# A new instruction order for a two-layer attention and feed-forward kernel: first norm's root on GpSimd, two stores on ScalarE, one more unit with its own silu table

## The chip, the cores and the metric

The kernel runs on one core of a Trainium2 chip. A core has five engines that run their own instruction streams: TensorE (PE, matrix products; PEld is its weight loads), VectorE (DVE), ScalarE (ACT, activation functions read from tables), GpSimd (POOL) and SyncE (SP, which here issues DMA transfers). They meet at semaphores. The metric is device time in microseconds (us), the median of a few runs.

## The reference

Two layers, applied one after the other to an input of 4 batches, 1024 tokens and 128 features. In both, x becomes x + attention(norm(x)) * silu(feed-forward(norm(x))).

- Layer norm: subtract the mean, divide by the root of the variance plus 1e-5.
- First attention: 16 heads of 8 features, a causal window of 64 tokens, scores q k / sqrt(128) plus a slope per head times distance, softmax, weighted values.
- First feed-forward: 8 experts are mixed per batch. A small gate network gives 8 factors, averaged over the tokens; the two weight matrices (128 x 512 and 512 x 128) and their biases are a base plus the factor-weighted sum of 8 expert matrices; between them stands a tanh-approximated gelu.
- Second attention: over the 4 batches at each token position, 16 heads, with a position bias scaled by a gate, softmax, output projection.
- Second feed-forward: silu(x W1 s1) * (x W2 s2), then two 512 x 512 layers with an exact gelu each, then back to 128 features; the weights are ternary and every output has a scale.

```
x = x + attention0(layernorm(x)) * silu(experts(layernorm(x)))
x = x + attention1(layernorm(x)) * silu(ternary_ffn(layernorm(x)))
```

## The kernel before

**Units.** The first layer's work is cut into eight units of 512 tokens, numbered in the order in which they are worked: `UNITS = ((0, 0), (0, 1), (1, 0), (1, 1), (2, 0), (3, 0), (2, 1), (3, 1))`, batch and half. The second feed-forward works on units of the same kind; the second attention on slices of 128 positions over all four batches.

**Order.** Every step is a small function that emits instructions for one or a few engines, registered under a short name. The string `ORDER` lists the steps as words: `s.02` is step `s` with arguments 0 and 2. A loop calls them in that order, and each engine executes its own instructions in the order in which they were emitted. Nothing reorders them later; what an engine waits for is settled by the buffers that its instructions read and write. The strings in `PLACES` say which buffer of a ring each tile gets, in order of use.

**Two parts.** A bar in `ORDER` divides it. The words ahead of the bar are the prologue: the whole attention of unit 0, and a test (`VN`, `CK`, `VP`, `VF`) whose result is a flag that all engines read before a branch. Behind the branch stands the same remainder twice, for a fast form and an exact form; the runs take the fast form. The remainder is called the body here.

**The prologue's steps.** `ls` takes statistics, `lp` the reciprocal root, `n` scales, `k` transposes on TensorE, `K` copies to the normalised input (ScalarE). `0` is a matmul on zeros that keeps TensorE running. `q` makes query, key and value products, `m` and `M` write four masked copies of the query (first 128 columns, then the rest, on ScalarE), `kc` stores the keys, `kp` the keys and values of the unit before (POOL), `v` stores the values (DVE). `s` makes a tile of scores in PSUM, for which there is a single buffer that the query product shares; `x` is the exponential on ScalarE, `o` weighs the values, `c` copies, `p` transposes, `d` divides. `A`, `AR`, `B`, `BP`, `C` make the gate factors, `D` and `H`/`HD` the mixed biases, `E` adds one expert matrix to the mixed weights (DVE). `RW` makes two small row weights for that bias. `CK.0` to `CK.3` sum the low bits of the ternary weights, one on DVE and three on ScalarE; their data come by DMA at the start.

**The body's steps.** `f`, `F`, `g`, `G`, `GS`, `r` are the first feed-forward, its silu and the residual. `T` loads expert weights from HBM (SP queue), `L.1` loads the second half of x, and SP issues in written order. `wa`, `wb` are the two gated products of the second feed-forward; `W` the activation, `U` and `V` the products around it, `WH`, `WL` its split in two parts; `ha`, `hb`, `hg`, `hH`, `hL` the first square layer, `ia`, `ib`, `ig`, `gH`, `gL` the second, `j` and `J` the output and its silu. `a` to `ay` are the second attention, `jt`, `y`, `Y` turn the gate, multiply, add and store.

**Tables.** ScalarE's functions lie in sets, and an activation from another set needs a load first. Exp and Tanh stand in the same set here; Silu, exact Gelu and the tanh-approximated Gelu each have another. A unit outside `DIRECT` computes silu from Tanh and one more DVE product (`U`); a unit in `DIRECT` uses Silu and has no `U`.

```
DIRECT = (3, 6, 7)
...
            if u in DIRECT:
                ACT.activation(sl, made["pw1", u, c], AF.Silu, scale=v("w1s", c))
                return
            ACT.activation(sl, made["pw1", u, c], AF.Tanh, scale=halved[:, 0, c:c + 1])
```

Of the kernel before, what the change touches and what calls it, by code (L numbers as in the profile page):

```python
# [52 lines left out]
def constants():  # L53
# [26 lines left out]
    0. ls.00 lp.00 n.00 0. ls.10 0. 0. k.00 0. K.00 q.0 m.00 m.03 m.02 M.00 m.01 M.03 lp.10 VN. M.01 kc.0 M.02 n.10 FI.  # L80
    CK.0 A.00 k.10 RW. v.01 kp.0 v.00 s.00 K.10 x.00 A.01 AR.01 AR.00 v.02 B.0 s.01 H.0 BP.0 o.00 C.0 CK.3 E.00 E.01
    E.02 E.03 E.04 ls.30 lp.30 D.0 x.01 s.02 o.01 CK.1 x.02 HD.0 s.03 n.30 E.05 CK.2 c.01 p.01 VP. x.03 E.06 o.02 VF.
    E.07 o.03 c.03 k.30 d.01 K.30 p.03 d.03 | T.00 f.10 f.00 ls.20 F.00 lp.20 T.01 q.1 f.11 n.20 F.10 L.1 T.10 kp.1 m.10
    f.01 kc.1 k.20 v.10 F.11 m.13 F.01 f.02 A.11 K.20 A.10 F.02 AR.11 T.12 f.12 m.11 m.12 f.03 E.08 E.09 E.0a E.0b E.0c
    AR.10 s.10 E.0d E.0e f.13 v.11 B.1 E.0f ls.60 F.12 F.03 BP.1 g.00 g.01 C.1 lp.60 T.11 x.10 v.12 s.11 E.10 n.60 F.13
    E.11 g.10 G.0 o.10 T.13 x.11 GS.0 E.12 E.13 s.12 E.14 E.15 E.16 E.17 x.12 T.14 g.11 r.0 ls.40 o.11 S.1 E.18 s.13
    c.11 G.1 f.20 x.13 lp.40 ls.01 p.11 lp.01 o.12 o.13 E.19 k.60 D.1 d.11 T.15 E.1a n.01 F.20 c.13 S.0 n.40 f.21 E.1b
    k.01 K.60 T.16 q.2 K.01 XH.0 F.21 f.30 ls.70 A.21 E.1c kc.2 m.20 m.22 k.40 E.1d T.24 F.30 AR.21 m.21 kp.2 XL.0 K.40
    f.31 T.17 lp.70 F.31 m.23 f.22 F.22 A.20 AR.20 ls.50 n.70 f.23 F.23 E.1e f.32 v.20 E.1f v.22 wa.00 p.13 F.32 lp.50
    B.2 W.00 wa.01 T.25 S.2 W.01 s.20 d.13 T.20 U.00 wb.00 U.01 BP.2 wb.01 C.2 f.33 V.00 wa.02 x.20 V.01 v.21 F.33 H.1  # L90
    E.20 s.21 W.02 HD.1 o.20 wa.03 E.28 E.21 U.02 GS.1 wb.02 n.50 W.03 V.02 g.20 wb.03 S.4 x.21 WH.00 WH.01 T.21 E.29
    r.1 g.21 U.03 V.03 E.22 T.22 E.23 G.2 k.50 s.22 WH.02 WH.03 k.70 WL.00 x.22 ha.00 K.70 o.21 E.24 T.26 E.25 E.2a c.21
    s.23 K.50 p.21 ha.01 x.23 GS.2 WL.01 WL.02 kp.3 o.22 o.23 c.23 d.21 ls.11 E.2b WL.03 hb.00 hg.00 hH.00 hb.01 hg.01
    q.3 hH.01 hL.00 S.3 hL.01 ha.02 hb.02 m.30 m.31 kc.3 p.23 m.33 m.32 hg.02 A.31 d.23 hH.02 v.31 hL.02 r.2 E.2c s.30
    v.30 g.30 ls.21 AR.31 A.30 x.30 AR.30 ha.03 hb.03 lp.21 s.31 hg.03 B.3 BP.3 v.32 T.30 n.21 E.2d C.3 U.30 g.31 lp.11
    E.30 k.21 T.34 x.31 K.21 o.30 hH.03 G.3 s.32 x.32 XH.2 XL.2 hL.03 o.31 n.11 wa.20 W.20 T.23 wa.21 E.26 wa.22 U.60
    c.31 U.20 W.21 W.22 s.33 o.32 p.31 E.27 x.33 U.21 U.22 wb.20 ia.00 d.31 wb.21 kp.4 o.33 GS.3 V.20 T.27 wa.23 WH.20
    E.31 V.21 c.33 ib.00 E.38 W.23 WL.20 ig.00 E.39 gH.00 T.35 U.23 WH.21 q.4 D.2 T.31 gL.00 ia.01 kc.4 p.33 ib.01 m.40
    m.42 m.43 m.41 wb.22 d.33 WL.21 ig.01 H.2 v.40 U.61 r.3 HD.2 v.42 s.40 x.40 wb.23 V.22 WH.22 gH.01 V.23 ia.02 ib.02
    s.41 WH.23 v.41 H.3 x.41 gL.01 L.2 WL.22 ig.02 ia.03 HD.3 ha.20 E.32 WL.23 E.3a ib.03 ig.03 hb.20 s.42 hg.20 E.2e  # L100
    E.2f o.40 E.33 T.32 hH.20 E.3b hL.20 o.41 gH.02 gL.02 gH.03 x.42 ha.21 ha.22 hb.21 D.3 gL.03 hb.22 T.33 c.41 ha.23
    hg.21 E.34 E.35 hb.23 ls.31 s.43 hH.21 hg.22 hH.22 hL.21 o.42 hg.23 j.00 hL.22 hH.23 hL.23 p.41 f.40 E.36 x.43 d.41
    j.01 z. j.02 T.36 E.37 lp.31 f.41 o.43 F.40 F.41 T.37 kp.5 c.43 U.70 j.03 f.42 q.5 F.42 J.00 kc.5 m.50 f.50 f.43
    v.50 v.52 F.50 m.52 n.31 F.43 g.40 k.31 g.41 m.51 ia.20 m.53 K.31 E.3c G.4 s.50 GS.4 p.43 ia.21 v.51 x.50 ib.20 E.3d
    ig.20 d.43 gH.20 r.4 ia.22 ls.41 gL.20 ib.21 ig.21 ib.22 ig.22 gH.21 gL.21 o.50 gH.22 gL.22 lp.41 s.51 f.51 f.52
    F.51 n.41 F.52 E.3e f.60 F.60 E.3f k.41 K.41 f.61 F.61 f.62 f.63 F.62 f.53 XH.4 XL.4 F.63 wa.40 W.40 F.53 g.50 x.51
    U.40 wb.40 g.51 V.40 G.5 wa.41 U.62 wa.42 W.41 U.41 W.42 U.42 s.52 wa.43 wb.41 x.52 V.41 wb.42 V.42 W.43 o.51 WH.40
    s.53 c.51 o.52 WH.41 WH.42 WL.40 wb.43 U.43 V.43 WL.41 WL.42 ia.23 x.53 p.51 o.53 GS.5 d.51 WH.43 WL.43 a.00 c.53
    ib.23 aq.00 p.53 kp.6 av.00 ig.23 d.53 gH.23 gL.23 r.5 q.6 ha.40 m.60 k.11 K.11 hb.40 ha.41 kc.6 hg.40 hH.40 m.62
    m.63 hb.41 hg.41 m.61 j.20 v.61 j.21 j.22 j.23 ls.51 lp.51 hL.40 n.51 v.60 hH.41 k.51 hL.41 J.20 K.51 XH.5 s.60 v.62  # L110
    g.60 XL.5 g.61 x.60 wa.50 W.50 wa.51 W.51 s.61 o.60 x.61 U.50 U.51 wa.52 G.6 wb.50 wb.51 V.50 V.51 s.62 wb.52 W.52
    WH.50 wa.53 U.52 a.01 WL.50 V.52 WH.51 WL.51 aq.01 wb.53 x.62 WH.52 W.53 av.01 XH.1 s.63 x.63 U.53 a.02 V.53 ha.42
    XL.1 wa.10 aq.02 av.02 W.10 U.10 hb.42 ha.43 wb.10 hb.43 V.10 hg.42 WL.52 hH.42 hL.42 hg.43 hH.43 o.61 wa.11 WH.53
    hL.43 W.11 a.03 WL.53 U.31 aq.03 ia.40 ib.40 WH.10 U.11 av.03 ag.0 c.61 ig.40 aG.0 wa.12 ap.0 W.12 wa.13 o.62 U.12
    o.63 kp.7 ia.41 W.13 U.13 ib.41 ia.42 gH.40 gL.40 GS.6 as.0 ib.42 ig.41 gH.41 ia.43 gL.41 ib.43 ig.42 gH.42 gL.42
    ig.43 gH.43 a.10 aq.10 av.10 ha.50 hb.50 p.61 gL.43 hg.50 hH.50 c.63 ha.51 hb.51 hg.51 d.61 hH.51 hL.50 p.63 hL.51
    d.63 q.7 a.11 v.71 WL.10 ae.0 ha.52 kc.7 hb.52 v.70 a.12 m.70 m.73 av.11 aq.11 hg.52 ha.53 hb.53 m.71 an.0 m.72
    aq.12 av.12 r.6 hH.52 a.13 ls.61 hg.53 ad.00 lp.61 s.70 hL.52 n.61 av.13 aq.13 j.40 x.70 j.41 ad.01 j.42 wb.11 v.72
    j.43 hH.53 V.11 hL.53 ag.1 s.71 wb.12 U.32 x.71 ia.50 WH.11 o.70 ap.1 V.12 s.72 aG.1 x.72 wb.13 ib.50 as.1 o.71
    WH.12 WL.11 c.71 s.73 V.13 o.72 ae.1 an.1 ad.02 ia.51 WH.13 XH.3 ib.51 x.73 ad.03 a.21 ig.50 ad.10 gH.50 ad.11 a.20  # L120
    ig.51 ad.12 av.20 p.71 o.73 WL.12 d.71 av.21 gH.51 gL.50 a.22 a.23 aq.20 gL.51 aD.10 XL.3 ad.13 wa.30 W.30 f.70
    aD.11 wa.31 ia.52 aq.21 aq.22 J.40 W.31 aq.23 wb.30 ag.2 ib.52 av.22 f.71 c.73 ig.52 a.30 ia.53 av.23 f.72 ap.2 F.70
    F.71 ib.53 gH.52 f.73 av.30 V.30 p.73 aG.2 at.1 as.2 aD.01 gL.52 F.72 F.73 g.70 aD.00 WL.13 ig.53 g.71 aq.30 wa.32
    wb.31 WH.30 a.32 at.0 gH.53 d.73 G.7 W.32 V.31 gL.53 wb.32 a.50 V.32 GS.7 ae.2 a.31 aq.50 av.50 a.33 wa.33 aq.31
    aq.32 j.50 j.51 ha.10 j.52 W.33 ha.11 an.2 WL.30 av.31 r.7 ls.71 WH.31 ad.20 j.53 aq.33 WH.32 J.50 ad.21 ha.12 av.32
    ad.22 av.33 a.40 hb.10 hb.11 lp.71 hg.10 k.61 ad.23 ag.3 ha.13 n.71 ap.3 hH.10 av.40 hg.11 hH.11 K.61 hb.12 wb.33
    hb.13 aq.40 hL.10 hL.11 hg.12 a.51 a.41 XH.6 aT.1 hH.12 aG.3 a.42 hg.13 V.33 hL.12 aq.51 k.71 hH.13 av.41 hL.13
# [20 lines left out]

DIRECT = (3, 6, 7)


LAST = (7, 3)
# [4 lines left out]

PLACES = {  # L160
    "big": (
        "0123456781234065782103645708325764125376087641376254734170182658734287401652858215874871530216153602"
        "74815703626850741"
    ),
    "ps_M": (
# [982 lines left out]
```

## Time and profile before

| | |
|---|---|
| time, median of 3 runs | 413.28 us (412.82 to 413.73) |
| the profiled execution | 415.04 us, of which the span from first to last instruction is 413.2 |
| granted TensorE clock, mean | 0.987 |
| PE, ScalarE, DVE, POOL busy | 398.1, 351.5, 325.7, 167.7 us |
| table loads on ScalarE | 71 of 1.283 us |
| read from HBM, written | 23.52 MB, 2.10 MB |

The page gives the busy time of each engine as a share of the span, the chain of work that ended last, and groups of instructions by source line: how many, the busy time, the mean time of one in ns, and the idle time of the engine just before them with what ended it. A timeline line has the start in us from the span's beginning, the duration, the engine, line, operation and tiles, and in brackets the idle time before. Because matmuls are pipelined, a busy PE is not PE at its peak. Times in the text are from the span's start unless something else is said. The branch lies between 32 and 36 us.

### The profile page before, as it was taken

Reading aid. Unit: us, or ns where it says so; the run is one execution under the profiler, and the core shown is the slowest. Engines: PE = TensorE matmul, PEld = TensorE weight load, DVE = VectorE, ACT = ScalarE, POOL = GpSimd, SP = SyncE. Lnnn points to the kernel's source line nnn. Section 1 sums busy time; section 2 is a strip of 40 time slices with the busy share of each in tenths; the row PEclk is TensorE's granted clock in tenths of the full one; section 3 lists DMA queues with packets and bytes.
Section 4 is the critical chain, followed back from the end, with each engine's and each line's share of the span. In section 5 each row is a group of like instructions: output and inputs, shape, how many; then the busy total and the mean of one; then the engine's idle time right before and its main releaser. Section 6 shows DMA issues by size and latency. Waiting matters only on the chain.

```text
span 413.2 us, 11394 instructions
## 1 busy us (share of the span) xinstructions
PE 398.1 (96%) x4800; PEld 283.2 (69%) x4800; DVE 325.7 (79%) x703; ACT 351.5 (85%) x491; POOL 167.7 (41%) x186
## 2 busy tenths in 40 slices
PE   7879999999999999999999999999999999999992
PEld 3446576577777676767777677666787776778881
DVE  6786989897679776653465596999899999999992
ACT  2875997999989999998988988878996999976972
POOL 2101034437422520031633362447556572675472
PEclk9978999999999999999999999999999999999997
DMA  8916663323114160000000000000000000000013
GB/s 282 389 62 216 243 195 117 102 103 116 43 54 149 36 205 3 2 2 2 2 2 3 2 2 0 2 3 2 2 0 1 2 1 0 2 0 27 0 72 116
DMA packets 8892, 26.43 MB, mean 64 GB/s; under 512 B 1248, under 2 KB 2048, under 8 KB 8448
## 3 DMA queue, kind: packets, MB, share of 16 engines
q1 hardware_dynamic: 8112, 23.79, 16.6%
q10 hardware_dynamic: 720, 1.84, 1.2%
q8 instruction: 39, 0.64, 0.7%
q14 instruction: 21, 0.17, 0.1%
HBM read 23.52 MB, written 2.10 MB: 62 GB/s over the span
## 4 chain that ended last, share of the span: by engine, by line
PE 79%; DVE 11%; ACT 4%; issue 3%; POOL 1%; DVEq 0%; POOLq 0%; ACTq 0%
PE ps_M L826 21%; PE ps_S L614 8%; PE ps_O L667 7%; PE ps_M L710 7%; PE ps_M L727 7%; PE ps_M L770 6%; PE ps_M L919 3%; PE ps_M L866 3%; PE ps_S L604 3%; DVE big L813 2%; PE ps_V L546 2%; PE ps_M L364 2%; PE ps_S L543 2%; PE ps_M L544 2%; DVE vb L971 2%
## 5 line engine op out<-in xcount | busy, mean ns | idle before, releaser
L826 PE MATMUL ps_M<-big,l1h 128*128 128x512 f32 x512 | 134.1, 405 | 0.6 <-DVE big L813 0.3
L826 PEld LDWEIGHTS ps_M<-big,l1h 128*128 128x128 f32 x512 | 93.8, 188 | 25.4 <-issue 3.2
L652 ACT ACTIVATE big<-ps_S 128x2048 f32<-128x2048 f32 x32 | 60.3, 1884 | 12.0 <-PE ps_S L614 11.5
L813 POOL TENSOR_TENSOR big<-t2k,big 128x512 fp32r<-128x512 f32 x32 | 42.3, 1332 | 57.1 <-ACT big L802 51.4
L813 DVE TENSOR_TENSOR big<-ps_M,big 128x512 fp32r<-128x512 f32 x63 | 42.4, 684 | 15.8 <-ACT big L842 11.3
L614 PE MATMUL ps_S<-big,k 32*64 32x256 f32 (+1 forms) x768 | 37.3, 472 | 1.1 <-issue 1.1
L527 DVE SCALAR_TENSOR_TENSOR mw<-tw,gr,mw 128x512 f32<-128x512 f32 x42 | 36.2, 871 | 1.8 <-DMA tw<-in_tw 1.5
L667 PEld LDWEIGHTS ps_O<-big,vb 128*32 128x32 f32 x2048 | 31.3, 113 | 8.4 <-issue 5.1
L667 PE MATMUL ps_O<-big,vb 128*32 128x64 f32 x2048 | 35.6, 225 | 0.0
L428 POOL TENSOR_TENSOR rstd<-rstd,power 128x4 f32<-128x4 f32 x15 | 15.5, 1032 | 49.1 <-DVE rstd L427 34.7
L1005 POOL TENSOR_TENSOR big<-big 128x512 f32<-128x512 f32 x16 | 23.5, 1476 | 21.0 <-DVE big L995 21.0
L710 PE MATMUL ps_M<-xn,mw 128*128 128x512 f32 x64 | 31.5, 602 | 0.3 <-PE ps_M L684 0.3
L727 PEld LDWEIGHTS ps_M<-mw,big 128*128 128x128 f32 x256 | 30.0, 192 | 2.3 <-issue 2.0
L727 PE MATMUL ps_M<-mw,big 128*128 128x128 f32 x256 | 31.3, 277 | 0.0
L742 POOL TENSOR_TENSOR g<-g,s 128x512 f32<-128x512 f32 x8 | 10.2, 1278 | 51.4 <-DVE s L702 35.3
L770 PE MATMUL ps_M<-xh,l1w 128*128 128x512 f32 x64 | 30.4, 474 | 0.3 <-ACT t2k L781 0.3
L919 PE MATMUL ps_M<-wa,xn 128*128 128x416 f32 x64 | 27.2, 522 | 0.1
L614 PEld LDWEIGHTS ps_S<-big,k 32*64 32x64 f32 x768 | 18.9, 133 | 12.1 <-issue 9.4
L770 PE MATMUL ps_M<-xl,l1w 128*128 128x512 f32 x64 | 25.2, 393 | 0.0
L847 ACT ACTIVATE ps_M<-ps_M,vec 128x512 f32<-128x512 f32 x31 | 20.3, 666 | 5.5 <-PE ps_M L826 5.4
L717 ACT ACTIVATE big<-ps_M,mb 128x512 f32<-128x512 f32 x32 | 21.6, 694 | 2.6 <-PE ps_M L710 2.2
L836 ACT ACTIVATE ps_M<-ps_M,vec 128x512 f32<-128x512 f32 x32 | 21.3, 668 | 2.4 <-PE ps_M L826 1.8
(192 smaller groups left out, 830.2 us busy)
## 6 DMA issues: line engine op xcount, KB each, us to landing
tw<-in_tw SPq DMA_DIRECT2D x24, 512.0 KB, 4.0
big<-in_tw SPq DMA_DIRECT2D x2, 1024.0 KB, 5.8
out<-xn SPq DMA_DIRECT2D x7, 256.0 KB, 2.0
g<-in_l1h ACTq DMA_DIRECT2D x2, 512.0 KB, 6.6
g<-in_l1h SPq DMA_DIRECT2D x2, 512.0 KB, 7.4
x<-in_tw SPq DMA_DIRECT2D x2, 512.0 KB, 5.1
x<-in_x SPq DMA_DIRECT2D x1, 1024.0 KB, 5.0
x<-in_x ACTq DMA_DIRECT2D x2, 256.0 KB, 4.0
```

Source lines behind the costliest of these rows:

```text
L527: DVE.scalar_tensor_tensor(m, part, made["gr", b][:, e:e + 1], base if e == 0 else m, ALU.mult, ALU.add)
L614: PE.matmul(sp[rows, j, :, q0:q0 + n], lhsT=k[r, key:key + W], rhs=qm[r, :, t * P + q0:t * P + q0 + n], start=bool(exact), stop=bool(exact ...
L652: ACT.activation(pr, sp, AF.Exp)
L667: PE.matmul(op[32 * j:32 * j + 32, part, qs], lhsT=vb[:, col:col + 32], rhs=pr[:, j, g, qs], start=(odd + i + g == 0), stop=(odd + i + g = ...
L710: PE.matmul(hp, lhsT=made["mixed", b][0][:, c * P:(c + 1) * P], rhs=xn[:, b, cx], start=True, stop=True)
L717: ACT.activation(made["hid", u][:, c, :], made["f", u, c], AF.Gelu_apprx_tanh, bias=made["mixed", b][2][:, c:c + 1])
L727: PE.matmul(op[:, i, :], lhsT=hid[:, c, i * P:(i + 1) * P], rhs=m2[:, c * D:(c + 1) * D], start=(c + i == 0), stop=(c + i == FC + 2))
L770: PE.matmul(p, lhsT=wt[name][:, c * P:(c + 1) * P], rhs=m, start=(n == 0), stop=(n == len(both) - 1))
L813: engine.tensor_tensor(made[key + "l", u][:, c, :], made[key + "v", u, c], made[key + "h", u][:, c, :].bitcast(F32), ALU.subtract)
L826: PE.matmul(made[name, u, c], lhsT=wt[name][:, i, c * P:(c + 1) * P], rhs=m[:, i, :], start=(n + i == 0), stop=(last and i == FC - 1))
L919: PE.matmul(mp[:, 0:N_ALL], lhsT=xn[:, b, place(sl)], rhs=wa[:, 0:N_ALL], start=True, stop=True)
L1005: POOL.tensor_tensor(pv[:, t:t + 2, 0:2, :], pv[:, t:t + 2, 0:2, :], pv[:, t:t + 2, 2:4, :], ALU.add)
```

## The change

1. Step `lp` for unit (0, 0): a ScalarE square root and a DVE reciprocal give way to the form that all other units have, an addition on DVE and a power of -0.5 on POOL. The constant `eps` goes, and the first ScalarE instruction is a copy instead of a square root.
2. Step `kc` for unit 0 runs on ScalarE, and the two stores of step `RW` too; both were on DVE.
3. `DIRECT` gains unit 1, batch 0's second half. It is the fourth unit whose silu is read from its own table.
4. `ORDER` is new in both parts, and `PLACES` with it. The words are the same; `kp.1` moves from the body into the prologue.

```diff
-    0. ls.00 lp.00 n.00 0. ls.10 0. 0. k.00 0. K.00 q.0 m.00 m.03 m.02 M.00 m.01 M.03 lp.10 VN. M.01 kc.0 M.02 n.10 FI.
-    CK.0 A.00 k.10 RW. v.01 kp.0 v.00 s.00 K.10 x.00 A.01 AR.01 AR.00 v.02 B.0 s.01 H.0 BP.0 o.00 C.0 CK.3 E.00 E.01
-    E.02 E.03 E.04 ls.30 lp.30 D.0 x.01 s.02 o.01 CK.1 x.02 HD.0 s.03 n.30 E.05 CK.2 c.01 p.01 VP. x.03 E.06 o.02 VF.
-    E.07 o.03 c.03 k.30 d.01 K.30 p.03 d.03 | T.00 f.10 f.00 ls.20 F.00 lp.20 T.01 q.1 f.11 n.20 F.10 L.1 T.10 kp.1 m.10
+    0. ls.00 0. lp.00 0. VN. 0. n.00 ls.10 0. lp.10 k.00 K.00 CK.1 q.0 FI. kp.0 n.10 A.00 CK.0 m.00 m.03 M.02 v.00 m.02
+    v.02 m.01 kc.0 M.01 k.10 M.03 M.00 K.10 s.00 A.01 x.00 AR.00 AR.01 v.01 B.0 s.01 BP.0 CK.3 x.01 C.0 o.00 D.0 CK.2
+    E.00 E.01 ls.30 s.02 x.02 RW. lp.30 VP. E.02 E.03 kp.1 E.04 E.05 E.06 o.01 s.03 n.30 VF. c.01 x.03 p.01 o.02 o.03
+    k.30 E.07 d.01 c.03 H.0 HD.0 p.03 d.03 K.30 | f.10 ls.20 q.1 T.00 f.11 L.1 F.10 m.10 lp.20 kc.1 n.20 f.12 m.12 F.11
+    f.00 v.11 v.10 T.01 F.12 f.01 m.13 F.00 v.12 E.08 F.01 k.20 K.20 A.11 m.11 A.10 AR.11 E.09 E.0a s.10 E.0b AR.10 x.10
...
-DIRECT = (3, 6, 7)
+DIRECT = (1, 3, 6, 7)
...
-    eps = const.tile([P, 1], F32, tag="eps", name="eps")
-    POOL.memset(eps, 1e-5)
...
-    ACT.activation(warm, one, AF.Sqrt)
+    ACT.copy(warm, one)
...
-            DVE.tensor_scalar(wb[:, 0, :], rp[:, 0, :], 1.0 / S, None, ALU.mult)
-            DVE.tensor_copy(wb[:, 1, :], rp[:, 1, :])
+            ACT.activation(wb[:, 0, :], rp[:, 0, :], AF.Copy, scale=1.0 / S)
+            ACT.copy(wb[:, 1, :], rp[:, 1, :])
...
             rstd = made["rstd", u, i] = small([P, 4], "rstd")
-            if (u, i) == (0, 0):
-                ACT.activation(rstd, made["mv", u, i][:, :, 1], AF.Sqrt, bias=eps)
-                DVE.reciprocal(rstd, rstd)
-                return
             (POOL if i else DVE).tensor_scalar(rstd, made["mv", u, i][:, :, 1], 1e-5, None, ALU.add)
             POOL.tensor_tensor(rstd, rstd, power, ALU.pow)
...
         def keys_of(u):
+            if u == 0:
+                ACT.activation(keys[:, W:W + U], made["kp", u], AF.Copy, scale=1.0 / math.sqrt(D))
+                return
             DVE.tensor_scalar(keys[:, W:W + U], made["kp", u], 1.0 / math.sqrt(D), None, ALU.mult)
```

## The prediction

> **What bounds the kernel now.** I read the page's busy shares and chain first, then the windows, then the timelines of TensorE and ScalarE up to 36 us.
>
> ```profile
> span 413.2 us, 11394 instructions
> PE 398.1 (96%) x4800; PEld 283.2 (69%) x4800; DVE 325.7 (79%) x703; ACT 351.5 (85%) x491; POOL 167.7 (41%) x186
> PE 79%; DVE 11%; ACT 4%; issue 3%; POOL 1%; DVEq 0%; POOLq 0%; ACTq 0%
> ...
> 13.17:16.58 3.41, 3.16 (x51) 1.84 (x50) 3.41 (x7) 3.07 (x6) 0.00 (x0) 1.00 1.04 387
> 16.58:19.99 3.41, 2.47 (x42) 0.95 (x42) 1.90 (x4) 3.41 (x6) 0.00 (x0) 1.00 1.04 407
> ...
> 23.41:26.82 3.41, 1.80 (x74) 1.22 (x70) 3.18 (x15) 1.98 (x3) 0.66 (x1) 1.00 0.03 7
> 26.82:30.23 3.41, 2.98 (x42) 1.47 (x42) 2.53 (x6) 2.00 (x5) 0.35 (x1) 0.50 0.02 5
> ...
> 200.00:250.00 50.00, 50.00 (x665) 37.22 (x666) 31.14 (x60) 44.01 (x61) 21.97 (x26) 1.00 0.01 2
> 280.00:340.00 60.00, 59.96 (x292) 44.29 (x281) 57.62 (x95) 53.84 (x91) 37.44 (x45) 1.00 0.00 1
> 340.00:370.00 30.00, 28.89 (x133) 21.63 (x132) 29.07 (x45) 26.66 (x45) 16.40 (x16) 1.00 0.00 1
> ```
> A window row gives its length, then the busy us of PE, PEld, DVE, ACT and POOL, then the granted clock. From about 36 us on PE has no gap worth having: 50.00 of 50 and 59.96 of 60, and 1.1 us missing at 340 to 370, where DVE is at 29.07 of 30. The matmuls are the same in number before and after. So the body can give about 1 us and can lose any amount. What can be won lies before 36 us.
>
> ```profile
> 5.88 1.28 ACT L323 ACT_TABLE_LOAD   x1 [5.88 <-DMA x<-in_x]
> ...
> 7.29 0.28 ACT L424 ACTIVATE rstd<-mv,eps 128x4 f32<-128x4 f32 x1
> 9.35 0.59 ACT L446 COPY xn<-ps_M 128x512 f32<-128x512 f32 x1 [1.78 <-PE ps_M L441]
> 11.15 0.89 ACT L581 ACTIVATE big<-ps_S,cst 128x128 f32<-128x128 f32 x3 [1.22 <-PE ps_S L543]
> ...
> 16.41 1.88 ACT L652 ACTIVATE big<-ps_S 128x2048 f32<-128x2048 f32 x1 [0.32 <-PE ps_S L614]
> ...
> 21.88 1.93 ACT L381 ACTIVATE big<-g 128x2048 f32<-128x2048 uint16 x1
> ...
> 25.32 1.88 ACT L652 ACTIVATE big<-ps_S 128x2048 f32<-128x2048 f32 x1 [1.43 <-PE ps_S L614]
> ...
> 30.02 1.88 ACT L652 ACTIVATE big<-ps_S 128x2048 f32<-128x2048 f32 x1 [1.41 <-PE ps_S L614]
> ```
> ```profile
> 24.62 0.65 PE L614 MATMUL ps_S<-big,k 32*64 32x256 f32 x5 [1.09 <-issue]
> ...
> 35.57 0.67 PE L710 MATMUL ps_M<-xn,mw 128*128 128x512 f32 x1 [0.31 <-PE ps_M L684]
> ```
> ```profile
> L652 ACT ACT_TABLE_LOAD x15 | 19.2, 1283 | 0.3
> L428 POOL TENSOR_TENSOR rstd<-rstd,power 128x4 f32<-128x4 f32 x15 | 15.5, 1032 | 49.1 <-DVE rstd L427 34.7 <-DVE shares L507 13.7
> L790 DVE SCALAR_TENSOR_TENSOR t2k<-t2k,ps_M 128x512 f32<-128x512 f32 x20 | 13.3, 682 | 9.4 <-ACT t2k L783 9.3
> ```
> The prologue is a ladder: four score tiles of the first unit, each through PE (about 1.65 us) and then ScalarE's exponential (1.88). The third and fourth exponentials wait 1.4 us each: the third because PE stood in the middle of its scores (24.62, released by nothing but issue), the fourth because PE's clock had been halved at 26.82. The first body matmul starts at 35.57.
>
> **The change, part by part.** *Root.* Before: table load to 7.16, root to 7.57, reciprocal, scaling at 7.81. After: DVE's add (0.17) ends near 5.8, POOL's power takes 1.03 (its row), scaling starts near 7.05. Those 0.76 us are mostly covered by the idle matmuls: five now stand ahead of the transposes instead of four, and the fifth is two warm passes of 0.43, so 7.57 becomes 8.43. Transposes (0.66) end at 9.1, and K.00 starts 0.23 earlier. POOL's second root moves to about 9.6 and is free at 10.7; its keys and value memsets follow, wanted at 15.
>
> *ScalarE's list.* Now K.00 (to 9.7), then CK.1 (row at 21.88: 1.8 and 0.2 for its read). Its data: issued at 2.11 and 7.4 to landing, about 9.5, just in time. It fills the 1.22 us in which ScalarE waited for the query, but costs 2.0: masks start at 11.75 instead of 11.15. Then four masks of 0.255, four of 0.475 and the keys (0.6 by the copy rows; DVE's row was 0.68): done at 15.4 instead of 14.2. The scores need the query's bank, so they wait for the last mask: 15.4, not 14.7. The first exponential starts at 17.1, 0.7 late. The Sqrt load and the Exp load at 14.80 merge into the one at 5.88, which saves 1.3 of ScalarE but nothing on the path, since the exponential waited for PE anyway.
>
> *PE's clock.* PE is idle from 13.9 (second transposes) to 15.4: 13.17 to 16.58 holds 0.73 + 1.18 = 1.91 us of matmuls, where before it held 3.16. The row 1.80 was followed by 0.50 for 6.8 us, the row 2.47 was not; 1.91 is nearest to 1.80, so I take half clock from 16.58 to 23.41. The Trainium skill ("TensorE: Matmul & The Clock Gate", "Why this matters for your kernels") asks only that there be no idle gap over about 3 us; by it nothing would halve here, and neither would it have at 26.82, where the longest gap was 1.5. The trace speaks against it; I keep both.
>
> *The ladder after.* Half clock (score tile 2.77 as at 27.25): exponentials at 17.55; 22.25 (bank free 19.4, two relus, CK.3); then CK.2 to 25.3; 25.85; row weights (2 x 0.28) and a copy; 29.45; then o.03 to 32.4, copy, last transposes 33.5, body from 33.85: 1.7 earlier than 35.57. Full clock: 17.1, 20.9, 24.5, 28.1, body from 32.4: 3.1 earlier. The gain is CK.1 out of the ladder's middle, and neither 1.4 us wait. DVE's share: gr at 22.6, eight expert steps of 0.75, stats, norm and flag to 32.6, still before 33.85. DVE loses the keys and row weights (1.25), which hid under PE.
> *Waits added.* The first scaling on DVE now waits for POOL instead of ScalarE; behind it stand the second half's statistics, whose root has until 10.7. The keys on ScalarE wait for the second projection (11.6, before their turn at 13.2); behind them stand three masks and the copy K.10. POOL's kp.1 copies come before the branch; their reads are over by 24.3, and only a later root stands behind them.
>
> *SP after the branch.* The 2 MB load of x now stands ahead of the second tw2 half, and waits for a DVE write behind one set of statistics, near 36. That half is issued near 36.4 instead of 33.41 and lands near 43.5 instead of 40.2 (the x load ahead of it took 5.0). Its first reader, expert step 0c, comes after some 8 us of DVE work from 36, near 44. Bounds 0 and +1; I take 0, as the second layer's weights are wanted only at g.00, later still.
>
> *Unit (0,1)'s silu.* Four DVE steps of 0.682 go (2.7 us); Tanh 0.687 becomes Silu 0.693. Built in order, the program has 73 table loads instead of 71, 72 of them in the body instead of 69: 3 x 1.283 = 3.85 us of ScalarE. A rule speaks against this: the skill ("ScalarE: Activation LUTs", "What ACT_TABLE_LOAD costs") adds a drain of about 1.38, 2.66 in all. Here the next activation follows its load by 1.30, so the row decides: 3.85, not 8.0. Most of it falls where unit (2,1) is scored, in the 200 to 250 row: ScalarE idle 50 - 44.0 = 6.0. 3.85 fits, 8.0 would not. I take 0 on the path, bounds 0 and +3.85. DVE's relief: at most the 1.1 us that PE lacks at 340 to 370; I take 0, since the four steps stood near 240, where DVE had slack.
> *Order otherwise.* Summing row means in written order, ScalarE's work never exceeds PE's over any stretch by more than 7.0 us (7.1 before), DVE's by 9.0 (11.1 before). I take 0, with bounds -1 and +3. Tail: six sums of 1.34 on POOL instead of five close together; the last is ready near the last multiply as before: 0.
>
> **Sum.** -0.2 (root and warm-up) and -1.5 (ladder) = -1.7. The profiled run took 415.04 (span 413.2 and 1.8 around), 1.8 above the median of 413.28; 1.7 off gives 413.3 profiled, 411.6 for the median.
>
> **The rivals.**
> *Full clock throughout:* the gap at 13.9 does not halve it. For: the page's rule, and 1.91 is over 1.80. Against: the row. -3.1: 410.2.
> *No change:* PE's stop at 24.62 returns. It reads as a late instruction, fetched while loads kept the DMA engines full to about 23; the same place in the program now comes near 24, after them. If it returns, 1.5 of the 1.7 is gone: 413.1.
> *Slower:* the extra loads reach PE. From unit (2,1)'s first exponential to its fourth ScalarE has 25.1 us of listed work against PE's 22.1; the same stretch before had 9.8 against 10.0. PE has a single score bank and cannot score until the exponential ends. It decides from the point where ScalarE enters this stretch less than 3 us ahead of need. For: three loads more, two of them here. Against: 6 us idle there, and a 7.1 excess near 55 us that cost nothing. With all 3.85 on PE: 413.28 - 1.7 + 3.85 = 415.4.
>
> **How the numbers follow.** Main case 0.36 (411.6), full clock 0.12 (410.2), no change 0.20 (413.1), slower 0.32 (415.4; an order this tight loses more easily than it wins). A measurement here tells 0.2%, 0.8 us, from no change. Faster 0.48, same 0.20, slower 0.32. Range 409.6 to 415.6: from full clock with half of DVE's 1.1 to the slower case. The main case alone: 410.5 to 412.4.
>
> **What would show it.** Right: 72 loads after the branch; first exponential near 17.1 to 17.6, third before 26, first body matmul 33 to 34.5; half clock moved to about 16.6; no long issue gap in the third scores; PE over 49.5 of 50 from 200 to 250. Wrong: first body matmul at 35 or later; PE idle behind exponentials or table loads after 200 us; DVE waiting near 44 for the second tw2 half.

## Result and the profile after

| | before | after |
|---|---|---|
| time, median | 412.76 us (412.00 to 413.73, 6 runs) | 415.10 us (414.41 to 415.71, 6 runs) |
| ratio | | 1.0053, 95% interval 1.0033 to 1.0072 |
| the profiled execution | 415.04, span 413.2 | 414.82, span 413.0 |

The changed kernel is slower by 0.5%, although its profiled execution was slightly faster than that of the kernel before. This contradiction leads to the first error of the prediction. One execution, of run 11 below, took 1244.73 us for a reason that the record does not show, and is left out of that run's ratio. First, the page and the window rows after, in the columns of the rows shown above (length, busy us of PE, PEld, DVE, ACT, POOL, granted clock, DMA):

```profile
span 413.0 us, 11393 instructions
PE 396.3 (96%) x4800; PEld 282.1 (68%) x4800; DVE 324.8 (79%) x696; ACT 352.7 (85%) x495; POOL 166.1 (40%) x186
```
```profile
8.05:11.46 3.41, 1.83 (x6) 1.04 (x7) 2.77 (x16) 1.41 (x2) 0.49 (x1) 1.00 1.04 402
11.46:14.88 3.42, 3.42 (x10) 2.00 (x9) 2.61 (x5) 3.42 (x9) 1.53 (x6) 0.50 1.05 334
...
200.00:250.00 50.00, 50.00 (x730) 37.35 (x721) 29.94 (x59) 48.01 (x64) 18.33 (x22) 1.00 0.01 2
...
280.00:340.00 60.00, 59.05 (x327) 44.20 (x326) 57.67 (x98) 50.44 (x89) 36.22 (x39) 1.00 0.00 1
340.00:370.00 30.00, 28.98 (x139) 23.50 (x138) 28.42 (x43) 27.91 (x47) 16.06 (x15) 1.00 0.00 1
```
The totals hardly move. The rows say more: the half clock is at 11.46 to 14.88 and nowhere near 16.58; from 200 to 250 TensorE is full although ScalarE took 4.0 us more there; from 280 to 340 it lacks 0.95 us where it had lacked 0.04. The timeline of ScalarE and TensorE after, at the rungs of the ladder:

```profile
10.05 0.59 ACT L440 COPY xn<-ps_M 128x512 f32<-128x512 f32 x1 [2.84 <-PE ps_M L435]
...
18.14 1.88 ACT L649 ACTIVATE big<-ps_S 128x2048 f32<-128x2048 f32 x1 [0.98 <-PE ps_S L611]
...
25.44 1.88 ACT L649 ACTIVATE big<-ps_S 128x2048 f32<-128x2048 f32 x1 [0.67 <-PE ps_S L611]
...
29.03 1.88 ACT L649 ACTIVATE big<-ps_S 128x2048 f32<-128x2048 f32 x1 [1.01 <-PE ps_S L611]
```
```profile
33.91 1.10 PE L707 MATMUL ps_M<-xn,mw 128*128 128x512 f32 x2 [0.44 <-DVE inv L693]
```
The first body matmul is 1.66 us earlier than the 35.57 of before, the size that was forecast (1.7). Yet the last product of the second feed-forward (`j`) ends at 405.58 instead of 404.82. Its lines, before and after:

```profile
403.80 1.02 PE L862 MATMUL ps_M<-t2k,l1w 128*128 128x512 f32 x2
```
```profile
404.55 1.02 PE L859 MATMUL ps_M<-t2k,l1w 128*128 128x512 f32 x2
```
So the body, counted from one to the other, took 371.67 us instead of 369.25: 2.42 more. Between these ends TensorE's gaps of over 60 ns add up to 3.21 us, before to 1.30. That is 1.91 of the 2.42; the gaps of 60 ns and less add up to 0.04 in both, so the other 0.5 us is not idle time of TensorE. The record does not say what it is. The longest gap after:

```profile
354.46 1.28 ACT L778 ACT_TABLE_LOAD   x1
...
355.76 0.69 ACT L778 ACTIVATE t2k<-ps_M,vec 128x512 f32<-128x512 f32 x1
...
356.50 0.50 PE L767 MATMUL ps_M<-xh,l1w 128*128 128x512 f32 x1 [1.02 <-ACT t2k L778]
...
357.04 1.28 ACT L844 ACT_TABLE_LOAD   x1
```
This is the silu of the last row tile of unit (3,1), `W.73`. One activation stands between two table loads, for gelu, silu and gelu again, and TensorE waits 1.02 us for the bank that this silu reads. The old order has the same single silu between two loads, before:

```profile
355.29 1.28 ACT L781 ACT_TABLE_LOAD   x1
356.63 0.69 ACT L781 ACTIVATE t2k<-ps_M,vec 128x512 f32<-128x512 f32 x1
357.34 1.28 ACT L836 ACT_TABLE_LOAD   x1
```
There TensorE has no gap behind it. What differs is not the pair of loads but what waits behind them.

### The profile page after: what moved, and what is told of

The parts are those of the page before. It is cut to its first block, busy times and chain, and to the rows that moved or that the text cites. A ratio compares the mean times of both kernels' runs of the same rounds, so it can differ in the third digit from the quotient of the medians.

```text
span 413.0 us, 11393 instructions
## 1 busy us (share of the span) xinstructions
PE 396.3 (96%) x4800; PEld 282.1 (68%) x4800; DVE 324.8 (79%) x696; ACT 352.7 (85%) x495; POOL 166.1 (40%) x186
## 3 DMA queue, kind: packets, MB, share of 16 engines
q10 hardware_dynamic: 720, 1.84, 1.3%
## 4 chain that ended last, share of the span: by engine, by line
PE 70%; DVE 15%; ACT 11%; issue 2%; POOL 0%; ACTq 0%; DVEq 0%
PE ps_M L823 19%; PE ps_M L767 7%; PE ps_S L611 6%; PE ps_M L724 6%; PE ps_M L707 6%; PE ps_O L664 6%; PE ps_M L916 2%; PE ps_S L601 2%; DVE big L810 2%; ACT big L649 2%; PE ps_M L863 2%; PE ps_V L540 2%; PE ps_M L538 2%; DVE big L992 2%; PE ps_S L537 2%
## 5 line engine op out<-in xcount | busy, mean ns | idle before, releaser
L823 PE MATMUL ps_M<-big,l1h 128*128 128x512 f32 x512 | 132.2, 402 | 0.0
L823 PEld LDWEIGHTS ps_M<-big,l1h 128*128 128x128 f32 x512 | 94.2, 188 | 24.6 <-issue 3.2
L422 POOL TENSOR_TENSOR rstd<-rstd,power 128x4 f32<-128x4 f32 x16 | 18.8, 1175 | 51.5 <-DVE rstd L421 50.8
L664 PEld LDWEIGHTS ps_O<-big,vb 128*32 128x32 f32 x2048 | 29.9, 110 | 10.2 <-issue 6.7
L611 PE MATMUL ps_S<-big,k 32*64 32x256 f32 (+1 forms) x768 | 35.8, 462 | 0.0
L521 DVE SCALAR_TENSOR_TENSOR mw<-tw,gr,mw 128x512 f32<-128x512 f32 x42 | 35.0, 847 | 0.3
L664 PE MATMUL ps_O<-big,vb 128*32 128x64 f32 x2048 | 34.2, 220 | 0.6 <-ACT big L649 0.6
L739 POOL TENSOR_TENSOR g<-g,s 128x512 f32<-128x512 f32 x8 | 11.4, 1428 | 46.7 <-ACT g L734 34.6
L833 ACT ACTIVATE ps_M<-ps_M,vec 128x512 f32<-128x512 f32 x32 | 21.3, 668 | 7.6 <-PE ps_M L823 7.3
L429 DVE TENSOR_SCALAR nt<-x,mv,rstd 128x128 f32<-128x128 f32 x64 | 20.4, 382 | 2.4 <-POOL rstd L422 2.4
```

The source lines that it names most:

```text
L521: DVE.scalar_tensor_tensor(m, part, made["gr", b][:, e:e + 1], base if e == 0 else m, ALU.mult, ALU.add)
L611: PE.matmul(sp[rows, j, :, q0:q0 + n], lhsT=k[r, key:key + W], rhs=qm[r, :, t * P + q0:t * P + q0 + n], start=bool(exact), stop=bool(exact ...
L664: PE.matmul(op[32 * j:32 * j + 32, part, qs], lhsT=vb[:, col:col + 32], rhs=pr[:, j, g, qs], start=(odd + i + g == 0), stop=(odd + i + g = ...
L823: PE.matmul(made[name, u, c], lhsT=wt[name][:, i, c * P:(c + 1) * P], rhs=m[:, i, :], start=(n + i == 0), stop=(last and i == FC - 1))
L833: ACT.activation(full, full, AF.Gelu, scale=v("h1s", c))
```

## Experiments

All ratios are to the kernel before, with 95% intervals. "Body" and "gaps" are read from each run's one profiled execution as above; the last digit can be off by one from rounding. The same words of the body differ between executions by up to 0.6 us (371.67 and 371.29 in the changed kernel and run 7, 369.91 and 370.49 in runs 10 and 11), so smaller differences of a body are not a result.

**1. The kernel before, once more.** No edit.

> The kernel before, unchanged, profiled a second time. Theory A: the first profiled execution (415.04 us) was an unlucky one, with the half clock at 26.82 and the stop at 24.62 in it, while the usual execution has neither; then this profile has its first body matmul near 33 us, not 35.57, and its span near 411. Theory B: the prologue always takes 35.6 us and the 1.8 us of the first profile lie elsewhere; then the first body matmul is again at 35 to 36. The ratio to itself is 1.000 within 0.2% in both.

Measured: 412.36 us, ratio 0.9994 (0.9975 to 1.0013). Its profiled execution took 412.41 with a span of 410.6, where the one used for the prediction had taken 415.04 and 413.2. Timelines and windows of this execution:

```profile
24.61 0.65 PE L614 MATMUL ps_S<-big,k 32*64 32x256 f32 x5 [1.10 <-issue]
...
33.44 1.95 PE L710 MATMUL ps_M<-xn,mw 128*128 128x512 f32 x4 [0.30 <-PE ps_M L684]
```
```profile
28.90 1.88 ACT L652 ACTIVATE big<-ps_S 128x2048 f32<-128x2048 f32 x1 [0.30 <-PE ps_S L614]
```
```profile
21.17:24.58 3.41, 1.94 (x70) 1.03 (x58) 3.27 (x5) 2.71 (x3) 0.00 (x0) 1.00 0.40 151
```
TensorE's stop at 24.6 is there again, so that one belongs to the kernel. The half clock behind it is not: the clock stays at 1.00, the fourth exponential starts at 28.90 instead of 30.02, and the first body matmul at 33.44 instead of 35.57. The body is 369.17, as it was. The prologue of this execution is thus 2.1 us shorter than that of the profile from which the prediction was worked out. It is also the more frequent kind: of 102 executions of the kernel before that were timed beside the twelve runs, 17 took over 414 us, all of them at a mean granted clock of 0.993 or less, and none of the 60 at 0.995 or more did.

**2. Old prologue, new body.** Against the kernel before, the places where the body begins:

```diff
-    E.07 o.03 c.03 k.30 d.01 K.30 p.03 d.03 | T.00 f.10 f.00 ls.20 F.00 lp.20 T.01 q.1 f.11 n.20 F.10 L.1 T.10 kp.1 m.10
+    E.07 o.03 c.03 k.30 d.01 K.30 p.03 d.03 | f.10 ls.20 q.1 T.00 f.11 L.1 F.10 kp.1 m.10 lp.20 kc.1 n.20 f.12 m.12 F.11
...
-DIRECT = (3, 6, 7)
+DIRECT = (1, 3, 6, 7)
```

> Prologue of before (words, places and code), body of the changed kernel with unit (0,1)'s own silu table. Theory A (the new body order loses, the new prologue gains nothing against the usual execution): ratio 1.004 to 1.006. Theory B (the body is equal and the new prologue loses): 0.999 to 1.001. Theory C (both lose about half): 1.002 to 1.003.

Measured: 415.38 us, ratio 1.0065 (1.0041 to 1.0090), just above theory A's range; body 371.80, with a wait of 1.03 us at 356.85.

**3. New prologue, old body.** Against the changed kernel, likewise:

```diff
-    k.30 E.07 d.01 c.03 H.0 HD.0 p.03 d.03 K.30 | f.10 ls.20 q.1 T.00 f.11 L.1 F.10 m.10 lp.20 kc.1 n.20 f.12 m.12 F.11
+    k.30 E.07 d.01 c.03 H.0 HD.0 p.03 d.03 K.30 | T.00 f.10 f.00 ls.20 F.00 lp.20 T.01 q.1 f.11 n.20 F.10 L.1 T.10 m.10
...
-DIRECT = (1, 3, 6, 7)
+DIRECT = (3, 6, 7)
```

> Prologue of the changed kernel (words, places, POOL root, keys and row weights on ScalarE), body of before, unit (0,1) by Tanh. Theory A: ratio 0.998 to 1.001. Theory B: 1.004 to 1.006. Theory C: 1.002 to 1.003. The forecast's own step, a prologue 1.7 us shorter, would be 0.996.

Measured: 413.09 us, ratio 1.0005 (0.9985 to 1.0025); body 369.26. Runs 2 and 3 together put the whole loss into the body: with the new one the time is that of the changed kernel, with the old one that of the kernel before, whichever prologue stands ahead.

**4. The own table alone, in the old order.**

```diff
-DIRECT = (3, 6, 7)
+DIRECT = (1, 3, 6, 7)
```

> The kernel before with only unit (0,1) added to those that read Silu from its own table: order and places as before, four DVE products fewer, the table loads that the old order then needs. If table loads of ScalarE reach TensorE: 1.28 us for each added load, ratio 1.006 or more for two or three added. If ScalarE's slack near 240 us hides them, as forecast: 0.999 to 1.001.

Measured: 417.79 us, ratio 1.0110 (1.0080 to 1.0141); body 374.64, 5.4 more. In the old order the own table costs more than the whole change does. ScalarE and TensorE at the place, and two windows:

```profile
241.46 1.28 ACT L781 ACT_TABLE_LOAD   x1
...
243.50 6.88 PE L826 MATMUL ps_M<-big,l1h 128*128 128x512 f32 x22 [1.89 <-ACT t2k L781]
```
```profile
240.70:244.11 3.41, 1.52 (x70) 1.26 (x59) 0.00 (x0) 3.37 (x6) 1.98 (x6) 1.00 0.02 5
244.11:247.53 3.42, 3.42 (x10) 2.65 (x9) 2.89 (x3) 1.57 (x3) 0.00 (x0) 0.50 0.00 0
```
The silu of the third row tile waits for a gelu's load, the gelu and its own load; TensorE stands for 1.89 us, and then 3.41 us pass at half clock, in which about 1.7 us of work is lost (3.41 times a half). The half clock belongs to this execution and not to the price: three of the six executions had a mean clock of 0.990 or 0.991 and took 417.32 to 418.01 us, the other three 0.996 or 0.997 and took 417.78 to 418.10. In every profile the clock is also halved for the last 2 to 5 us, so that 0.996 leaves no room for another step of 3.41. TensorE's gaps add up to 3.75 us here, 2.45 more than before; the rest of the 5.4 is not explained for the executions at whole clock.

**5. Tanh in the new order.**

```diff
-    W.10 a.03 WL.53 W.11 av.03 wa.12 c.61 aq.03 ia.40 W.12 x.63
+    W.10 U.10 a.03 WL.53 W.11 U.11 av.03 wa.12 c.61 aq.03 ia.40 W.12 U.12 x.63
...
-    wa.13 as.0 W.13 q.7
+    wa.13 as.0 W.13 U.13 q.7
...
-DIRECT = (1, 3, 6, 7)
+DIRECT = (3, 6, 7)
```

> Edit: the changed kernel with unit (0,1)'s silu back in the exponential's table (Tanh and four DVE steps, moved behind their Tanh in the written list); 72 table loads instead of 73. The body runs from the first body matmul to the last attention output; it was 369.25 us before and 371.67 after. Theory A (the own table is what costs in the new order, as it does in the old one, where it alone gave a ratio of 1.011): body back near 369.5, time near 413.0, ratio to before 1.000 to 1.002. Rival B (the new order itself costs it, wherever the silu takes its table): body 371 to 372, ratio 1.004 to 1.007, and the 1.02 us gap of TensorE at 356.5 is still there. A mixture would show the gap at 356.5 and a body near 370.5.

Measured: 415.71 us, ratio 1.0065 (1.0042 to 1.0089); body 372.99, gaps 3.82, and the 1.02 us at 358.05. Rival B's ratio and its gap hold, and the body is even above its 372: the new order costs this wherever the silu takes its table. The body is 1.3 us longer than with the own table; part of this may be the place of the four returned DVE steps, since TensorE waits for them twice (0.34 at 237.95, 0.18 at 251.74). This run also tells what the own table adds in the new order. It has 71 loads after the branch, the changed kernel 72, the kernel before 69: one load of the three belongs to the own table, and two come with the new order, wherever the silu takes its table.

**6. The last silu beside the third, in the new order.**

```diff
-    W.72 ay.2 aT.3 ig.30 V.71 wa.73 WH.70 WL.70 as.7 ia.31 ia.32 gH.30 ha.60 W.73 ad.40
+    W.72 wa.73 W.73 ay.2 aT.3 ig.30 V.71 WH.70 WL.70 as.7 ia.31 ia.32 gH.30 ha.60 ad.40
```

> Edit: the changed kernel with the last row tile's silu of unit (1,3) (words wa.73 and W.73) moved directly behind the third's, so that it shares its table; 71 loads instead of 73. Theory A (the 1.02 us gap of TensorE at 356.5, where this one activation stands between two table loads of its own, is part of the loss): the gap is gone, body 370.6, time near 414.0, ratio to before 1.002 to 1.004. Rival B (what that gap holds back is made up by slack later, or the two loads only move the wait on): body within 0.4 of 371.67, ratio 1.004 to 1.007, and other gaps stand between 350 and 380.

Measured: 413.61 us, ratio 1.0022 (1.0011 to 1.0033); body 370.43, 1.24 less than in the changed kernel, and no gap between 323 and 396:

```profile
340.00:370.00 30.00, 30.00 (x144) 24.32 (x143) 29.54 (x45) 25.79 (x44) 17.34 (x16) 1.00 0.00 1
```
Theory A holds. Two words moved take two loads away and give back about half of the loss.

**7. The halving behind the first scaling, in the new prologue.** In the changed kernel DVE's next work behind the first root is the word `VN`. The timeline of DVE in the changed kernel:

```profile
7.91 0.17 DVE L368 TENSOR_SCALAR halved<-vec 128x4 f32<-128x4 f32 x1 [1.90 <-DMA vec<-in_vec]
...
8.52 1.11 DVE L429 TENSOR_SCALAR nt<-x,mv,rstd 128x128 f32<-128x128 f32 x4
```
```diff
-    0. ls.00 0. lp.00 0. VN. 0. n.00 ls.10 0. lp.10 k.00 K.00
+    0. ls.00 0. lp.00 0. 0. n.00 VN. ls.10 0. lp.10 k.00 K.00
```

> Edit: the changed kernel with DVE's word that halves the vector (the one that waits 1.90 us for a transfer) moved behind the first scaling. Theory A (that wait is why the first scaling starts at 8.52 instead of the forecast 7.05): the scaling starts near 7.0 and the query copy on ScalarE near 9.3 to 9.6 instead of 10.05; if the chain behind it follows, the first exponential starts near 17.5 instead of 18.14, the first body matmul near 33.4 instead of 33.91, ratio to before 1.003 to 1.005. Rival B (the idle matmuls or the transfer of the keys' weights that ScalarE waits for hold the prologue anyway): first exponential within 0.2 of 18.1, first body matmul within 0.3 of 33.9, ratio 1.004 to 1.007.

Measured: 415.26 us, ratio 1.0060 (1.0039 to 1.0082); body 371.29. DVE's first scaling in this run:

```profile
6.88 1.11 DVE L429 TENSOR_SCALAR nt<-x,mv,rstd 128x128 f32<-128x128 f32 x4 [1.23 <-POOL rstd L422]
```
It now waits for the root, as the forecast had it (7.05); the first exponential starts at 17.19 and the first body matmul at 33.03. In its trace theory A holds. In the time nothing of it can be seen, and the ratio lies in rival B's range: the intervals of this run and of the changed kernel lie over each other, and 0.9 us of one execution's prologue is of the size by which executions differ.

**8. New prologue so mended, old body.** The edits of runs 3 and 7 together, with the body's three PSUM banks renamed (0 to 2, 1 to 0, 2 to 1). Against run 3:

```diff
-    0. ls.00 0. lp.00 0. VN. 0. n.00 ls.10 0. lp.10 k.00 K.00
+    0. ls.00 0. lp.00 0. 0. n.00 VN. ls.10 0. lp.10 k.00 K.00
```

> Edit: the new prologue with the halving moved as in the run before this one, and then the old body (Tanh for unit (0,1), old order), with the body's three PSUM banks renamed so that its first projection does not wait for the bank of the prologue's last product. Theory A (the old body is worth 369.25 wherever it starts, and the prologue ends earlier once its wait is gone): first body matmul near 33.0 to 33.4, body 369.3, ratio to before 0.996 to 0.999. Rival B (the new prologue cannot beat the old one in its usual execution): first body matmul 33.9 to 34.4 as it was, ratio 0.999 to 1.003.

Measured: 412.31 us, ratio 0.9984 (0.9964 to 1.0004); body 369.42, first body matmul 33.86. The body is as theory A had it; the start is as rival B had it, because this execution had half clock from 17.67 to 21.08. Undecided against the kernel before.

**9. Four more words of the new order.** Runs 6 and 7 together, and

```diff
-    ha.00 E.26 kc.3 hb.00 F.33 hg.00 T.30 r.2 ls.21 lp.21 m.30 v.30 v.31 hH.00 hL.00
+    ha.00 E.26 kc.3 hb.00 F.33 hg.00 T.30 r.2 ls.21 lp.21 v.30 v.31 hH.00 m.30 hL.00
...
-    r.4 ig.21 gL.20 gH.21 ls.41 ig.22 gH.22 o.50 f.50 lp.41 gL.21 f.61
+    r.4 ig.21 gL.20 gH.21 ig.22 gH.22 o.50 f.50 gL.21 ls.41 lp.41 f.61
...
-    K.61 wa.31 an.2 V.30 W.31 wb.31 g.71 V.31 wa.32
+    K.61 wa.31 V.30 W.31 wb.31 g.71 V.31 an.2 wa.32
...
-    j.53 W.60 ag.5 af.1 ag.4 WH.33 J.50 wa.61
+    j.53 W.60 J.50 ag.5 af.1 ag.4 WH.33 wa.61
```

> Edit: the changed kernel with the last row tile's silu of unit (1,3) early as before, the halving behind the first scaling, and four words moved so that no short work stands ahead of what TensorE waits for: m.30 behind hH.00, the statistics ls.41 behind gL.21, the normalisation an.2 behind V.31, the silu J.50 ahead of three words. They aim at the gaps of 0.26 (107), 0.33 (182), 0.24 (294) and 0.40 us (323), 1.23 in all. Theory A (the rest of the body's loss is the sum of these small waits): body 370.43 - 1.23 = 369.2, as in the old order; ratio to before 0.998 to 1.000. Rival B (waits only move on to the next word): body 370.0 to 370.6, ratio 1.001 to 1.003.

Measured: 412.64 us, ratio 1.0005 (0.9988 to 1.0022); body 369.82, 0.61 less than in run 6 where 1.23 had been aimed at. The gaps at 107, 294 and 323 are gone or smaller; the one at 182 grew from 0.33 to 0.51, and new ones of 0.12 and 0.33 stand at 110 and 114. Most of it moved on: the gaps counted in the whole body add up to 2.04 us, against 2.20 in run 6. The 0.61 of the body is no larger than the difference between two executions of one body, and the interval overlaps that of run 6. With all these moves the new order cannot be told from the old one; which of the last five brought the ratio from 1.0022 to 1.0005, if any, is open.

**10 and 11. Three words of the old body, with the new prologue and with the old.**

```diff
-    W.70 hH.32 WL.61 a.73 W.71 a.62
+    W.70 WL.61 a.73 W.71 hH.32 a.62
...
-    hg.60 hg.33 hH.33 aD.31 hL.33
+    hg.33 hH.33 hg.60 aD.31 hL.33
...
-    WL.71 an.5 aT.3 aU.3 ib.32 hL.62 af.3 jt.40
+    WL.71 aT.3 aU.3 ib.32 hL.62 an.5 af.3 jt.40
```

> Edit: the new prologue with the late halving and the old body with three words moved: hH.32 behind W.71, hg.60 behind hH.33, an.5 behind hL.62. They aim at the old body's gaps of 0.25 (342), 0.32 (353) and 0.20 us (365). Theory A (a gap of TensorE in the body is worth its length): body 369.42 - 0.77 = 368.7, ratio to before 0.996 to 0.998, under both kernels. Rival B (the waits move on): body 369.2 to 369.5, ratio 0.998 to 1.000.

> Edit: the kernel before with the same three words moved in its body, its prologue as it is. Theory A (the new prologue, with its halving late, is worth no more than the old one in its usual execution, and a gap is worth its length): body 368.5, first body matmul near 33.4, ratio to before 0.997 to 0.999, within 0.001 of the run with the new prologue. Rival B (the prologue's change is worth its 0.4 us or more, as the first body matmul at 33.03 in one execution suggests): this one stays 0.001 to 0.002 above that run.

Measured: with the new prologue 412.34 us, ratio 0.9988 (0.9974 to 1.0002), body 369.91; with the old 412.80 us, ratio 1.0002 (0.9986 to 1.0018), body 370.49. Both bodies are longer than the old one, which no theory had. Two of the three moves made the wait longer: 0.25 us at 342 became 0.44, and 0.32 at 353 became 1.59. Only the 0.20 at 365 is gone. ScalarE and TensorE at the place, in run 10:

```profile
349.18 1.28 ACT L833 ACT_TABLE_LOAD   x1 [1.95 <-PE ps_M L823]
```
```profile
352.54 0.73 PE L823 MATMUL ps_M<-big,l1h 128*128 128x512 f32 x2 [1.59 <-DVE big L810]
```
`hg.60` had been the first of the two gelus, its input was there early, and the load was made while the product for `hg.33` was still running. With `hg.33` first, the load itself waits for that product, 1.95 us, and the bank that the low half behind it gives back is late. The prologue's part agrees with the trace: in run 10 the exponentials start at 17.09, 20.80, 24.39 and 28.08 and the first body matmul at 32.76, in run 11 the latter is at 33.18. That would be 0.4 us for the new prologue; the two ratios lie 0.0014 apart with intervals that overlap, so it is not settled.

**12. The own table in the old order, with the four silus together.**

```diff
-    ag.0 c.61 ig.40 aG.0 wa.12 ap.0 W.12
+    ag.0 c.61 aG.0 wa.12 ap.0 W.12
...
-    ib.41 ia.42 gH.40 gL.40 GS.6 as.0 ib.42 ig.41 gH.41 ia.43 gL.41
+    ib.41 ia.42 GS.6 ig.40 gH.40 gL.40 as.0 ib.42 ig.41 gH.41 ia.43 gL.41
```

> Edit: the kernel before with unit (0,1)'s silu from its own table, and three words (the gelu ig.40, its high and low halves) moved behind the four silus and the small silu GS.6, so that these share one load: 72 loads instead of 74 (71 with Tanh). Theory A (the own table's price in the old order, 1.1%, is the wait of the silu behind a load and a gelu, with TensorE empty for 1.89 us at 243.5 and its clock halved in the 3.41 us that follow): gap and half clock are gone, body near 370.5, ratio 1.002 to 1.005. Rival B (the price is the loads themselves, ScalarE's time, wherever they stand): ratio above 1.007, and gaps of TensorE behind ScalarE elsewhere between 225 and 260.

Measured: 418.02 us, ratio 1.0137 (1.0105 to 1.0170), with two loads fewer than in run 4; body 373.43. TensorE and its window:

```profile
249.02 0.96 PE L919 MATMUL ps_M<-wa,xn 128*128 128x416 f32 x2 [2.52 <-DVE big L813]
```
```profile
247.22:250.63 3.41, 1.61 (x6) 1.15 (x7) 2.88 (x7) 0.70 (x2) 0.00 (x0) 1.00 0.00 0
```
In this execution the wait for the silu is gone, and so is the half clock. But DVE now begins `as.0` at 243.58, before the low half `gL.41`, which stands behind it in the order. Its input was cast by 244.18; DVE comes to it at 248.28, and TensorE waits for that bank: 2.52 us in place of 1.89. And this execution, 415.59 us at a mean clock of 0.997, is the fastest of six: the others took 416.96 to 420.61, longer mostly where the clock was lower, from 0.996 down to 0.984. At 0.996 and more run 12 took 415.59 and 416.96, run 4 417.78 to 418.10. So the grouping gained 1 to 2 us where the clock was whole, and lost it again to half clock that this one trace does not show. Theory A's range is missed; rival B has the ratio, but the long gap stands behind DVE and not ScalarE. That the price is the time for which some bank stays taken is a reading of these two traces, not a test of it.

## Why the prediction was wrong, point by point

**The profiled execution that the sum stood on was not the usual one.** This is the step that failed first. The prediction took 1.7 us off the profiled 415.04 and the same 1.7 off the median of 413.28, as if the 1.8 us between the two were the constant that lies outside the span. But 1.7 to 1.9 us lie outside the span in every execution (413.2 and 415.04; 410.6 and 412.41 in run 1), and the median contains them too. The profiled execution was itself slow: the half clock at 26.82 and most of the fourth exponential's wait of 1.41 (0.30 in run 1) were its own. Against the 33.44 of run 1 the changed kernel's 33.91 is no gain, and runs 2 and 3 show none in the time either. 415.04 lay outside the three runs shown (412.82 to 413.73); the question to ask was which row was its excess.

**The ladder's term had the right working and the wrong start.** The first exponential came at 18.14 instead of 17.55, the third before 26 (25.44). That the first body matmul came at 33.91, beside the 33.85 of the main case, is luck: the half clock of that case was not there, and the four exponentials follow the full-clock rival's steps (17.1, 20.9, 24.5, 28.1) about 1.0 us late. With the halving moved, run 10 follows this ladder within 0.11 us at each exponential, and its first body matmul is at 32.76 for the rival's 32.4.

**The root's term missed a wait.** The root itself was ready at 6.91, as forecast. But `VN`, a word that the diff puts ahead of `n.00`, waits 1.90 us for the vector's transfer, and the scaling started at 8.52 instead of 7.05. The forecast asked what waits behind the scaling and not what the new order puts in front of it.

**Half clock from 16.58 to 23.41 did not come.** It was taken because 1.91 us of matmuls is nearest to the 1.80 of one row. It came from 11.46 to 14.88 instead, behind the window of 1.83 that holds the wait for `VN`. The longest gap of TensorE ahead of 26.82, which the prediction gives as 1.5, is 1.09 by the line at 24.62. The last section returns to the clock.

**The own silu table at 0 had the loads wrong.** The prediction charges all three added loads, 3.85 us, to unit (0,1)'s silu. Run 5 shows that one of them is its own and two come with the order. For the one, 0 fits the trace: ScalarE is at 48.01 in 200 to 250, TensorE full, and the changed kernel is not slower than run 5. In the old order the own table does add three loads (69 to 72 after the branch), and the body is 5.4 us longer, outside the upper bound of 3.85. So neither a count of loads nor ScalarE's idle time gave the price; how it comes to 5.4 is explained only in part. DVE's relief was 0 where it was looked for: in run 4, without the four DVE steps, the old order's gaps of TensorE between 340 and 370 still add up to 1.08 us (1.11 before). The second half of `tw2` cost nothing: DVE's idle time at 44.30 is 0.69 us, and it waits for ScalarE.

**Order otherwise at 0 is the term that decided the sign.** The body measured +2.42 us, within the term's bound of +3. Runs 2, 3 and 5 put this into the order of the body; run 6 returns 1.24 of it with `W.73` beside the third silu. The rest is not pinned down. Gaps of a few tenths, as at 162 and 317, are part of it, 0.5 us of it are no gaps, and the moves of run 9 leave open which of them matter. The forecast compared sums of work over stretches, ScalarE's excess of 7.0 with 7.1 before. Such a sum is blind to the wait at 356.50: no engine is overfull there, one bank's reader stands behind one load too many.

**The rivals.** The slower case said 415.4, close to 415.1, but for another reason: its place, unit (2,1)'s exponentials between 200 and 250, shows no wait at all, and its 1.7 us of prologue gain does not exist against the usual kernel. "PE idle behind exponentials or table loads after 200 us" was named as what would show the forecast wrong, and the line at 356.50 is that. *No change* rested on TensorE's stop at 24.62. The stop is in all six profiles of the old prologue, always in the third scores (0.82 to 1.38 us). In five of the eight of the new one it stands among the row-weight products instead (0.27 to 1.01 us, at 24.85 to 26.31), behind the third scores, where the third exponential does not wait for it. In all eleven TensorE goes on 2.2 to 2.6 us after a transfer of 16 KB on the instruction queue begins (at 22.08 in the profile before). This fits the prediction's reading of a late instruction; no run tested it.

## What to carry to other kernels

Before working out a gain from a stretch of one profiled execution, set its time against the other runs; if it stands above them, find the row that is its excess and take it out first. For a reordered program whose bound engine has no slack, walk along the banks and ask for each who reads it last and what has been put ahead of that reader; sums over stretches don't see it. A table load is priced where it stands: one activation between two loads cost 1.02 us in the new order and nothing that TensorE shows in the old one.

## What the runs showed of the hardware

The granted clock moves in steps of 3.41 us, and the grid of the steps lies elsewhere in each execution: the half clock of the profile before began at 26.82, those of the changed kernel, run 4, run 8 and run 9 at 11.46, 244.11, 17.67 and 15.80. The step before each held little matmul: 1.80, 1.83, 1.52, 1.59 and 0.92 us of 3.41. Run 9's windows:

```profile
12.39:15.80 3.41, 0.92 (x6) 0.48 (x5) 2.40 (x3) 3.41 (x12) 0.00 (x0) 1.00 1.06 369
15.80:19.21 3.41, 3.19 (x41) 1.51 (x41) 1.89 (x3) 1.04 (x3) 0.00 (x0) 0.50 0.99 377
```
Steps on the execution's own grid with 1.94 (run 1), 1.77 (run 10), 1.80 (run 11) and 1.61 us (run 12) were not followed by half clock, so 1.6 to 1.8 us busy of 3.41 went either way in these traces. The longest idle gaps that reach into the steps ahead of the five half clocks were 1.09, 1.39, 1.89, 1.84 and 2.70 us; gaps of 2.28 (run 7) and 2.52 us (run 12) left the clock whole. What else decides is not shown. The Trainium skill ("TensorE: Matmul & The Clock Gate", "What's actually happening") states a free-running window of 3413 ns that does not start with the kernel. The steps agree with it, and with it in mind the half clock at 26.82 could have been read as one execution's luck: the same stop at 24.6 left the clock whole in run 1. The same page's rule of a gap of over about 3 us, which the prediction weighed, is too lenient for what these runs show.
